# Two intermediate tensors re-laid by six-channel groups across all images, and the last pass issued in halves instead of thirds

## The chip, the cores and the metric

The kernel runs on one core of one Trainium2 chip. Its metric is the device time of one execution in microseconds (us); the kernel before took a median of 6009.42 us in three runs (6007.35 to 6020.1).

## The reference

Two residual layers over an image batch `x` of shape (8, 96, 96, 192), all in float32. `_gn` is a group norm with 32 groups of six channels.

```python
# layer 0
proj  = x_gn @ W_in + b_in                      # 192 -> 384
local = conv3x3_depthwise(proj)
mixed = 0.25 * (lr + rl + tb + bt) + local      # four running means (s = 0.6 s + 0.4 x) over rows and columns
x     = x + layernorm(mixed) @ W_out + b_out    # 384 -> 192
# layer 1
y = conv7x7_depthwise(_gn(x)) + dw_bias
y = layernorm(y)
y = gelu(y @ w0 + b0) @ w1 + b1                 # 192 -> 768 -> 192
x = x + y * gamma
```

The output has the shape of `x`.

## The kernel before

The work runs in five stages, one after the other, with intermediate tensors in DRAM between them. The order of instructions on every engine is the order in which the code issues them; each stage is written out inside a manual schedule.

- **A, projection** (to line 528): group norm of `x` and the 192 to 384 projection; the result goes to `P_d`. On the side it prepares shifted copies of the convolution kernels (`Z1_d`, `Z2_d`) and writes one row of zeros (`pad`, line 298) behind the end of `X1_d`.
- **B, 3x3 convolution and running means** (lines 540 to 683); result in `M_d`.
- **C, layer norm and output projection** (lines 765 to 982): 192 steps `u`. `load_c` (line 807) loads `mt` and `xr` on SP's queue; `block_c` runs TensorE; `finish_c` (line 851) forms the new `x` (called x1), stores it in token order to `X2_d` on POOL's queue and copies it into `x1c`, in channel-major order. When sixteen steps are done, `x1c` holds, for two images and one of three column phases, 96 rows of all 192 channels; sixteen calls of `store_c` (line 926) write it to `X1_d` on SP's queue, twelve channels each, one call per following step. At the end one store is made, then `load_d(0)` is issued, and then the other fifteen stores.
- **D, 7x7 convolution** (lines 991 to 1083): sixteen groups `i` of twelve channels. A tile `m` holds six channels of all images for three pairs of row blocks: `load_d` (line 738) loads `xin`, its lower 64 partitions on SP's queue and its upper 64 on POOL's, and `band`, the shifted kernel, in the same way. Five tiles `xin` exist in turn. `scale_d` (line 1004) applies the second group norm on VectorE, eight instructions a tile. `conv_d` (line 1011) does the convolution as banded matmuls of 63 rows and 64 columns, four of them side by side in TensorE's array, and ScalarE adds the bias into `yo`. `store_d` (line 1043) writes `yo` to `Y_d` in sixteen transfers on POOL's queue (in the last group, the first image pair's part goes to SP's queue).
- **E, layer norm and the two-layer network** (lines 1093 to 1270): 96 units `u` of four columns of two images, 96 rows each. `load_y` (line 1113) loads `Y_d` on SP's queue once in four units; `load_r` (line 1118) loads the residual from `X2_d`; `stats_e` and `norm_e` are the layer norm on VectorE; `turn_in(u, k)` (line 1163) transposes on TensorE into `pt` and copies to `yT` on VectorE; `first_layer(u, mb)` (line 1177) multiplies with `w0w`; `second_layer(u, k)` (line 1209) multiplies with `w1g`, adds the residual on VectorE and stores to the output on POOL's queue.

The contraction over 192 channels in `first_layer` is done as one matmul over 128 rows (line 1186) and one over 64 rows (line 1196); the two halves of a unit's tokens use the upper and the lower 64 rows at the same time. ScalarE then applies GELU (line 1205). Each call of `first_layer` does two of six output blocks, `ms = (2 * mb, 2 * mb + 1)`, and so four PSUM tiles `hp`. PSUM is shared out as two `pt`, four `hp` and two `po`.

The order of E around the change, for each unit `u`:

```python
for k in range(3):
    first_layer(u, k)
    turn_in(u + 1, k)
    ...                      # loads, statistics and norm of u + 2 on VectorE
    second_layer(u - 1, k)
```

The layouts that the change touches: `X1_d` is (image pair, row and column phase; channel; column; image of the pair), so that one partition of `xin` reads four runs of 1536 bytes, one per image pair. `Y_d` is (row and phase; image pair, half; channel; column and image), so that one partition of `yo` writes eight runs of 768 bytes, and one partition of `y` reads one run of 24,576 bytes.

Of the kernel before, what the change touches and what calls it, by code (L numbers as in the profile page):

```python
# [8 lines left out]
F32 = mybir.dt.float32  # L9
# [75 lines left out]
def conv_blocks_kernel(  # L85
# [31 lines left out]
    nc = tc.nc  # L117
# [24 lines left out]

    X1_d = dram.tile([BP * S * PH + 1, D, WV, 2], F32, name="X1_d")
    X2_d = dram.tile([BP, PH, S, WV, 2, D], F32, name="X2_d")
    NV = 2
    WQ = WV // NV

    Y_d = dram.tile([S * PH, BP, NV, D, 2 * WQ], F32, name="Y_d")

# [71 lines left out]
    with ExitStack() as ph:  # L221
# [30 lines left out]
        k1t = zp.tile([S, 2, 7, 7], F32, name="k1t")  # L252
        pad = zp.tile([S, D * WV * 2 // S], F32, name="pad")

# [35 lines left out]
        def store_kernels():  # L290
            nc.sync.dma_start(
                Z0_d.rearrange("(m p) t l -> p m (t l)", p=128),
                z0.rearrange("p m t l -> p m (t l)"),
            )

            nc.sync.dma_start(Z1_d.rearrange("(i c) p l -> c i p l", c=S), z1)
            nc.sync.dma_start(
                X1_d[BP * S * PH].rearrange("(i c) v b -> i (c v b)", i=S), pad
            )
# [430 lines left out]
    HG = HB - 6  # L730
    HC = GS
    CD = 2 * HC
# [5 lines left out]
    def load_d(m):  # L738
        c = m * HC
        row = D * WV * 2  # L740
        pool = d_pools[m % ND > 0]
        xin = pool.tile([128, NT, BP, HC, 2 * WV], F32, tag="xin", name="xin")

        for t in range(NT):
            for g, eng in enumerate((nc.sync, nc.gpsimd)):
                src = bass.AP(
                    tensor=X1_d.tensor,
                    offset=X1_d.offset + (2 * t + g) * HG * PH * row + c * WV * 2,
                    ap=[[row, 64], [S * PH * row, BP], [1, HC * WV * 2]],
                )  # L750
                eng.dma_start(
                    xin[g * 64 : (g + 1) * 64, t].rearrange("q a c n -> q a (c n)"), src
                )
        band = pool.tile([128, HC, ZW], F32, tag="band", name="band1")
        for g, eng in enumerate((nc.sync, nc.gpsimd)):
            eng.dma_start(
                band[g * 64 : (g + 1) * 64].rearrange("q c l -> q (c l)"),
                Z2_d[:, c : c + HC].rearrange("r c l -> r (c l)"),
            )
        return band, xin  # L760
# [4 lines left out]
    with ExitStack() as ph:  # L765
# [160 lines left out]
        def store_c(x1c, k, q):  # L926
            c = slice(q * D // NX, (q + 1) * D // NX)
            bp, p = divmod(k, NH)
            r = bp * S * PH
            nc.sync.dma_start(X1_d[r + p : r + S * PH : PH, c], x1c[:, c])  # L930

# [59 lines left out]
    with ExitStack() as ph:  # L991
# [51 lines left out]
        def store_d(yo, i):  # L1043
            for bl in range(NB):
# [6 lines left out]
                for k in range(2):  # L1051
                    c = i * CD + k * HC
                    for lo, hi in pieces:
                        r = (S - HB - bl * HG) * PH
                        src = yo[k * 64 + lo * PH : k * 64 + hi * PH, bl]
                        dst = Y_d[r + lo * PH : r + hi * PH, :, :, c : c + HC].rearrange(
                            "r b a c n -> r (b a) (c n)"
                        )
                        src = src.rearrange("r a c n -> r a (c n)")

                        n = NV if i == D // CD - 1 else 0
                        if n:
# [28 lines left out]


    WH = 4
    WE = 2 * WH
    HE = 128 // WH
    with ExitStack() as ph:
        ip = ph.enter_context(tc.tile_pool(name="e_in", bufs=2))
        sp = ph.enter_context(tc.tile_pool(name="e_small", bufs=3))
        tp = ph.enter_context(tc.tile_pool(name="e_t", bufs=2))
        ps_t = ph.enter_context(tc.tile_pool(name="e_ps_t", bufs=2, space=PSUM))  # L1100
        ps_h = ph.enter_context(tc.tile_pool(name="e_ps_h", bufs=4, space=PSUM))
        ps_o = ph.enter_context(tc.tile_pool(name="e_ps_o", bufs=2, space=PSUM))

# [9 lines left out]
        def load_y(n):  # L1113
            bp, p, a = place(n)
            ys[n] = ip.tile([S, D, 2 * WQ], F32, tag="y", name=f"y_{n}")
            nc.sync.dma_start(ys[n], Y_d[PH - 1 - p :: PH, bp, a])

# [59 lines left out]
        def first_layer(u, mb):  # L1177
            if mb == 0:
                gs[u] = tp.tile([128, NE, 2, WH * S], F32, tag="g", name="g")
            yT, g = yTs[u].rearrange("p k h j -> p k (h j)"), gs[u]  # L1180
            ms = (2 * mb, 2 * mb + 1)
            hps = {}
# [26 lines left out]
        def second_layer(u, k):  # L1209
            if k == 0:  # L1210
                xos[u] = tp.tile([128, S // HE, 2, D], F32, tag="xo", name="xo")
            g, xo = gs[u], xos[u]
            po = ps_o.tile([128, 2, D], F32, tag="po", name="po")
            for q in range(2):
# [24 lines left out]
        with tc.manual_schedule():  # L1239
# [10 lines left out]
            for u in range(n_u + 1):  # L1250
                for k in range(3):
                    if u < n_u:
                        first_layer(u, k)
                    if u + 1 < n_u:
                        turn_in(u + 1, k)
                    if k == 0:
                        if u + 1 < n_u:
                            load_r(u + 1)
                        if u < n_u:
                            bias_r(u)  # L1260
                    if u + 2 < n_u:
                        if k < 2:
                            for j in range(4 * k, 4 * k + 4):
                                stats_e(u + 2, j)
                        else:
                            for j in range(WE):
                                norm_e(u + 2, j)
                    if u >= 1:
                        second_layer(u - 1, k)

# [46 lines left out]
```

## Time and profile before

The profiled execution took 6011.68 us, its span (first to last instruction) 6009.9 us. The three runs have a median of 6009.42 us.

| engine | busy us | share of the span |
|---|---|---|
| TensorE matmul (PE) | 5680.5 | 95% |
| TensorE weight load (PEld, beside PE) | 3943.4 | 66% |
| VectorE (DVE) | 3454.0 | 57% |
| POOL | 2634.7 | 44% |
| ScalarE (ACT) | 2440.3 | 41% |

| stage | us from the span's start | us |
|---|---|---|
| A | 0 to 782 | 782 |
| B | 782 to 1835 | 1053 |
| C | 1835 to 2924 | 1089 |
| change-over from C to D | 2924 to 3014 | 90 |
| D | 3014 to 3501 | 487 |
| from D to E | 3501 to 3546 | 45 |
| E and its tail | 3546 to 6010 | 2464 |

The stages' bounds are read off TensorE's timeline, so they are good to a few us. How to read the views that follow: a *group* line gives source line, engine, operation, output<-input and how often; a *wait* line says who waited for whom, total us, times, longest; a *timeline* line gives the start, the time and a run of like instructions, and in brackets how long the engine was idle before it and what ended that. TensorE is pipelined, so the distance between starts says more than the busy time. `X_d` in the profile stands for both `X1_d` and `X2_d`. DMA transfers go through queues: q0 is POOL's, q1 is SP's; all queues share sixteen DMA engines.

### The profile page before, as it was taken

To read this page: it belongs to the slowest core of one execution; us is meant where nothing else is said; L and a number is where in the kernel's file an instruction comes from. 1 tells how busy PE (TensorE), PEld (TensorE's weight loads), DVE (VectorE), ACT (ScalarE), POOL (GpSimd) and SP (SyncE) were. 2 spreads that over 40 slices of the span, in tenths; PEclk is the share of its full clock that TensorE was granted. 3 is DMA by queue.
4 is the path that set the end of the run, shared out by engine and by line. 5 is a ranking of instruction groups with operands and counts; after the bars stand their busy time and mean duration, and the time that the engine had idled before them with its cause. 6 is when DMAs were issued, how large, how long until landed. Compare 5 with 4: busy or idle time off the path is not lost.

```text
span 6009.9 us, 122810 instructions
## 1 busy us (share of the span) xinstructions
PE 5680.5 (95%) x48550; PEld 3943.4 (66%) x48550; DVE 3454.0 (57%) x8023; ACT 2440.3 (41%) x6146; POOL 2634.7 (44%) x2835
## 2 busy tenths in 40 slices
PE   6999989999998999999677769999999999999999
PEld 3655633333336989898666657777777777777777
DVE  5555469999995667777532334444444444444442
ACT  2444457777774555555333322222222222222221
POOL 1111148888886666666444422322332233233222
PEclk9999989999999999999888889999999999999999
DMA  7999779999987888888899952222222222222221
GB/s 206 282 285 258 219 213 243 244 242 244 244 231 210 266 261 268 262 267 261 232 286 290 284 141 69 66 72 63 79 64 78 64 79 64 78 64 77 61 64 37
DMA packets 570206, 1054.36 MB, mean 175 GB/s; under 512 B 109575, under 2 KB 426260, under 8 KB 567328
## 3 DMA queue, kind: packets, MB, share of 16 engines
q1 hardware_dynamic: 439344, 593.23, 37.8%
q0 software_dynamic: 124160, 450.67, 24.1%
q8 instruction: 384, 6.29, 0.5%
q10 hardware_dynamic: 6128, 2.61, 0.2%
q14 instruction: 190, 1.56, 0.1%
HBM read 585.19 MB, written 476.57 MB: 177 GB/s over the span
## 4 chain that ended last, share of the span: by engine, by line
PE 77%; DMA 6%; DVE 1%; issue 1%; SPq 1%; POOL 1%; ACT 0%; DVEq 0%; POOLq 0%; ACTq 0%
PE po L1216 19%; PE po L833 13%; PE hp L1186 12%; PE pl L579 10%; PE hp L1196 7%; PE pa L600 5%; PE pt L831 4%; DMA xin<-X_d 4%; PE py L1024 2%; PE pt L1169 2%; PE pa L603 2%; DMA Y_d<-yo 1%; DVE xin L1009 1%; DMA band<-Z_d 0%; SPq L1063 0%
## 5 line engine op out<-in xcount | busy, mean ns | idle before, releaser
L1205 ACT ACTIVATE g<-hp,b0g 128x384 f32<-128x384 f32 x1152 | 573.9, 580 | 1856.4 <-PE hp L1196 1856.4
L1216 PE MATMUL po<-w1g,g 128*128 128x192 f32 x6912 | 1178.3, 327 | 0.0
L1216 PEld LDWEIGHTS po<-w1g,g 128*128 128x128 f32 x6912 | 1116.6, 190 | 1.6 <-issue 1.1
L833 PE MATMUL po<-wc,mt 128*96 128x193 f32 x4608 | 912.8, 333 | 0.0
L1173 DVE COPY yT<-pt 128x384 f32<-128x384 f32 x288 | 251.4, 873 | 1126.7 <-PE pt L1169 1126.4
L1234 POOL DMA_DIRECT2D out_dram<-xo x576 | 321.3, 560 | 1147.9 <-DVE xo L1223 1119.4
L1186 PE MATMUL hp<-yT,w0w 128*128 128x384 f32 x2304 | 794.4, 488 | 0.4 <-ACT g L1205 0.4
L833 PEld LDWEIGHTS po<-wc,mt 128*96 128x96 f32 x4608 | 701.8, 163 | 68.6 <-ACT mean L837 65.0
L579 PE MATMUL pl<-pin,band 34*32 34x380 f32 (+1 forms) x13824 | 629.9, 489 | 19.3 <-DMA pin<-P_d 18.5
L1186 PEld LDWEIGHTS hp<-yT,w0w 128*128 128x128 f32 x2304 | 431.4, 191 | 231.6 <-issue 2.6
L609 DVE TENSOR_TENSOR_SCAN z<-decay,loc 128x768 f32<-128x768 f32 x288 | 505.9, 1756 | 61.2 <-ACT loc L588 31.7
L1024 PE MATMUL py<-xin,band 63*64 63x248 f32 (+1 forms) x6912 | 405.5, 394 | 138.3 <-DVE xin L1009 136.2
L649 POOL TENSOR_TENSOR mo<-mo,z 128x768 f32<-128x768 f32 x288 | 529.6, 1839 | 3.3 <-ACT mo L604 0.4
L618 DVE TENSOR_TENSOR_SCAN z<-decay,z 128x768 f32<-128x768 f32 x288 | 498.2, 1730 | 0.0
L579 PEld LDWEIGHTS pl<-pin,band 34*32 34x32 f32 x13824 | 232.8, 107 | 398.7 <-issue 397.1
L1024 PEld LDWEIGHTS py<-xin,band 63*64 63x64 f32 x6912 | 345.0, 142 | 198.5 <-DVE xin L1009 123.5
L840 ACT ACTIVATE sq<-pt,mean 96x384 f32<-96x384 f32 x768 | 443.0, 577 | 25.7 <-ACT mean L837 0.8
L1196 PE MATMUL hp<-yT,w0w 64*128 64x384 f32 x2304 | 449.4, 508 | 0.0
L600 PE MATMUL pa<-loc,mix 128*32 128x384 f32 x3456 | 431.9, 493 | 0.0
L603 PE MATMUL pa<-last,down 96*32 96x384 f32 x1152 | 426.9, 493 | 0.9 <-ACT mo L604 0.9
L29 POOL TENSOR_TENSOR rs<-rs_ve,neg_half 96x8 f32<-96x8 f32 x96 | 158.6, 1652 | 606.3 <-DVE rs_ve L28 606.3
L362 PE MATMUL pm<-xT,win 128*128 128x384 f32 x1152 | 395.9, 494 | 3.3 <-DVE po L386 3.3
(116 smaller groups left out, 7707.4 us busy)
## 6 DMA issues: line engine op xcount, KB each, us to landing
P_d<-po POOLq DMA_DIRECT2D x96, 1152.0 KB, 9.9
pin<-P_d SPq DMA_DIRECT2D x192, 576.0 KB
mt<-M_d SPq DMA_DIRECT2D x576, 192.0 KB
xq<-in_x_dram SPq DMA_DIRECT2D x96, 576.0 KB
xr<-in_x_dram SPq DMA_DIRECT2D x384, 144.0 KB
X_d<-x1u POOLq DMA_DIRECT2D x192, 288.0 KB, 4.2
X_d<-x1c SPq DMA_DIRECT2D x192, 288.0 KB
y<-Y_d SPq DMA_DIRECT2D x24, 2304.0 KB
```

The lines of the kernel that those rows point to most:

```text
L579: nc.tensor.matmul(pls[g][at * RB : (at + 1) * RB, :, lo:hi], band[rows, c, kh, :], pin[rows, c, :, NJ - 1 - j, lo + kh - 1 : hi + kh - 1] ...
L600: nc.tensor.matmul(pa[at], mix[:, i, at], loc[:, q], start=True, stop=True)
L603: nc.tensor.matmul(pa[at], down[:, to], last[:, q], start=True, stop=True)
L609: nc.vector.tensor_tensor_scan(zf, decay_f, loc.rearrange("p q n -> p (q n)"), 0.0, ALU.mult, ALU.add)
L618: nc.vector.tensor_tensor_scan(zr, decay_f, zr, 0.0, ALU.mult, ALU.add)
L649: nc.gpsimd.tensor_tensor(m, m, z, ALU.add)
L833: nc.tensor.matmul(po[:S, b], lhs[m], wc[:, m], start=(m == 0), stop=(m == NC - 1))
L1024: nc.tensor.matmul(pys[t // 2][g][k * 64 : (k + 1) * 64, t % 2, :, lo:hi], pair[k][0][rows, c, d * ZS : d * ZS + 64], pair[k][1][rows, t, ...
L1186: nc.tensor.matmul(hps[m, q], w0w[:, 2 * q, m * 128 : (m + 1) * 128], yT[:, 2 * q], start=True, stop=False,)
L1196: nc.tensor.matmul(hps[m, q], w0w[p, 1, m * 128 : (m + 1) * 128], yT[p, 1], start=False, stop=True,)
L1205: nc.scalar.activation(g[:, m, q], hps[m, q], AF.Gelu, bias=b0g[:, m : m + 1], scale=1.0)
L1216: nc.tensor.matmul(po[:, q], g[:, m, q, k * 128 : (k + 1) * 128], w1g[:, m], start=(m == 0), stop=(m == NE - 1),)
```

## The change

Both intermediate tensors get the layout (row and phase; group of six channels; image pair; ...), so that for one row and one group of six channels the values of all images lie together in DRAM, 6144 bytes. A tile `xin` then reads one run of 6144 bytes per partition, and `yo` writes one. `store_c` writes two runs of 1536 bytes per row where it wrote one of 3072, and `load_y` reads 32 runs of 768 bytes per partition. The numbers of transfers and the bytes stay as they were, except for the row of zeros, which is four times as long.

In the last pass `first_layer` does three of the six output blocks in a call and is called twice a unit, not three times. PSUM is shared out anew: one `pt`, and seven buffers in turn for both `hp` and `po`. The order per unit is written out by hand: first half, transposes 0, second layer 0, transposes 1, second half, transposes 2, second layer 1, second layer 2.

```diff
-    X1_d = dram.tile([BP * S * PH + 1, D, WV, 2], F32, name="X1_d")
+    HC = GS
+    X1_d = dram.tile([S * PH + 1, D // HC, BP, HC, WV, 2], F32, name="X1_d")
...
-    Y_d = dram.tile([S * PH, BP, NV, D, 2 * WQ], F32, name="Y_d")
+    Y_d = dram.tile([S * PH, D // HC, BP, NV, HC, 2 * WQ], F32, name="Y_d")
...
-        pad = zp.tile([S, D * WV * 2 // S], F32, name="pad")
+        pad = zp.tile([S, D * WV * B // S], F32, name="pad")
...
-        row = D * WV * 2
+        row = D * WV * B
...
-                    offset=X1_d.offset + (2 * t + g) * HG * PH * row + c * WV * 2,
-                    ap=[[row, 64], [S * PH * row, BP], [1, HC * WV * 2]],
+                    offset=X1_d.offset + (2 * t + g) * HG * PH * row + c * WV * B,
+                    ap=[[row, 64], [1, HC * WV * B]],
...
-            r = bp * S * PH
-            nc.sync.dma_start(X1_d[r + p : r + S * PH : PH, c], x1c[:, c])
+            nc.sync.dma_start(
+                X1_d[p : S * PH : PH, c.start // HC : c.stop // HC, bp].rearrange(
+                    "h g c v b -> h g (c v b)"
+                ),
+                x1c[:, c].rearrange("h (g c) v b -> h g (c v b)", c=HC),
+            )
...
-                        dst = Y_d[r + lo * PH : r + hi * PH, :, :, c : c + HC].rearrange(
-                            "r b a c n -> r (b a) (c n)"
+                        dst = Y_d[r + lo * PH : r + hi * PH, c // HC].rearrange(
+                            "r b a c n -> r (b a c n)"
                         )
-                        src = src.rearrange("r a c n -> r a (c n)")
-
-                        n = NV if i == D // CD - 1 else 0
+                        src = src.rearrange("r a c n -> r (a c n)")
+
+                        n = NV * HC * 2 * WQ if i == D // CD - 1 else 0
...
-        ps_t = ph.enter_context(tc.tile_pool(name="e_ps_t", bufs=2, space=PSUM))
-        ps_h = ph.enter_context(tc.tile_pool(name="e_ps_h", bufs=4, space=PSUM))
-        ps_o = ph.enter_context(tc.tile_pool(name="e_ps_o", bufs=2, space=PSUM))
+        ps_t = ph.enter_context(tc.tile_pool(name="e_ps_t", bufs=1, space=PSUM))
+        ps_h = ph.enter_context(tc.tile_pool(name="e_ps_h", bufs=7, space=PSUM))
...
-            nc.sync.dma_start(ys[n], Y_d[PH - 1 - p :: PH, bp, a])
+            nc.sync.dma_start(
+                ys[n].rearrange("h (g c) n -> h g (c n)", c=HC),
+                Y_d[PH - 1 - p :: PH, :, bp, a].rearrange("h g c n -> h g (c n)"),
+            )
...
-            ms = (2 * mb, 2 * mb + 1)
+            ms = range(mb * NE // 2, (mb + 1) * NE // 2)
...
-            po = ps_o.tile([128, 2, D], F32, tag="po", name="po")
+            po = ps_h.tile([128, 2, D], F32, tag="hp", name="po")
...
-                for k in range(3):
-                    if u < n_u:
-                        first_layer(u, k)
-                    if u + 1 < n_u:
-                        turn_in(u + 1, k)
...
-                    if u >= 1:
-                        second_layer(u - 1, k)
+                if u < n_u:
+                    first_layer(u, 0)
+                if u + 1 < n_u:
+                    turn_in(u + 1, 0)
+                    load_r(u + 1)
+                if u < n_u:
+                    bias_r(u)
+                if u + 2 < n_u:
+                    for j in range(4):
+                        stats_e(u + 2, j)
+                if u >= 1:
+                    second_layer(u - 1, 0)
+                if u + 1 < n_u:
+                    turn_in(u + 1, 1)
+                if u < n_u:
+                    first_layer(u, 1)
+                if u + 1 < n_u:
+                    turn_in(u + 1, 2)
+                if u + 2 < n_u:
+                    for j in range(4, WE):
+                        stats_e(u + 2, j)
+                if u >= 1:
+                    second_layer(u - 1, 1)
+                if u + 2 < n_u:
+                    for j in range(WE):
+                        norm_e(u + 2, j)
+                if u >= 1:
+                    second_layer(u - 1, 2)
```

## The prediction

> **What bounds the kernel now.** I first read the profiled execution by stage, as a table of engine busy time in stretches: projection, 3x3 convolutions, output projection with the norm (C), then the change-over into the 7x7 convolution, that convolution (D), its end, and the last pass (E) with its tail.
>
> ```profile
> 1835.00:2924.00 1089.00, 1074.75 (x6931) 972.98 (x6932) 752.94 (x2657) 630.95 (x2300) 720.94 (x577) 0.99 0.87 259
> 2924.00:3014.00 90.00, 35.34 (x474) 31.68 (x474) 41.38 (x123) 13.86 (x29) 19.80 (x32) 0.66 0.89 225
> 3014.00:3501.00 487.00, 379.58 (x6476) 321.65 (x6476) 134.37 (x225) 188.23 (x359) 218.57 (x342) 0.87 1.01 278
> 3501.00:3546.00 45.00, 3.29 (x13) 2.09 (x14) 9.26 (x28) 0.68 (x2) 11.16 (x17) 0.52 0.86 202
> 3546.00:5978.00 2432.00, 2426.43 (x12548) 1808.30 (x12549) 1112.38 (x2944) 573.23 (x1149) 722.13 (x757) 1.00 0.24 68
> ```
>
> Columns: stretch and its us, busy time of PE, PEld, DVE, ACT and POOL, TensorE clock, DMA share, GB/s. C and E are TensorE's (1075 of 1089 us, 2426 of 2432). D is not: TensorE is busy 380 of 487 us, at a clock of 0.87, and the DMA engines are full at 278 GB/s.
>
> For D I read the waits and then one period in the timelines of POOL, DVE and PE.
>
> ```profile
> DVE xin L1009 <- DMA xin<-X_d: 329.3, 28, 23.4
> PE py L1024 <- DVE xin L1009: 109.5, 15, 10.7
> POOL Y_d L1064 <- DMA xin<-X_d: 75.1, 56, 2.5
> ```
> ```profile
> 3206.60 0.70 POOL L1064 DMA_DIRECT2D Y_d<-yo  x1 [2.83 <-ACT yo L1035]
> ...
> 3230.46 1.31 POOL L751 DMA_DIRECT2D xin<-X_d  x2 [0.76 <-PE py L1024]
> ```
> ```profile
> 3244.91 4.74 DVE L1009 TENSOR_SCALAR xin<-xin,s 128x576 f32<-128x576 f32 x8 [20.75 <-DMA xin<-X_d]
> ```
> ```profile
> 3216.65 24.78 PE L1024 MATMUL py<-xin,band 63*64 63x256 f32 x432 [9.74 <-DVE xin L1009]
> 3249.71 25.23 PE L1024 MATMUL py<-xin,band 63*64 63x256 f32 x432 [8.28 <-DVE xin L1009]
> ```
>
> TensorE loses 8 to 10 us before each group of twelve channels, because a group's second tile arrives late. The convolution before last ended at 3206.9. Its 16 stores are first in POOL's queue and take until 3230.5, since each POOL transfer waits for the eighth before it (the built program shows eight semaphores used in turn); only then does POOL ask for its half of the next tile, which is there at 3244.9; DVE normalizes for 4.8; TensorE starts at 3249.7. So 23.6 + 14.4 + 4.8 = 42.8 us from one end to the start after next, with a convolution of 25 inside: (42.8 + 25)/2 = 33.9 us per group, against 33.1 measured.
>
> For E I read TensorE's timeline in the steady state.
>
> ```profile
> 4011.38 2.74 PE L1186 MATMUL hp<-yT,w0w 128*128 128x384 f32 x8
> 4014.06 1.56 PE L1196 MATMUL hp<-yT,w0w 64*128 64x384 f32 x8
> 4015.55 0.55 PE L1169 MATMUL pt<-ident,yn 96*128 96x96 f32 x4
> 4015.93 4.09 PE L1216 MATMUL po<-w1g,g 128*128 128x192 f32 x24
> 4019.86 0.49 PE L1186 MATMUL hp<-yT,w0w 128*128 128x384 f32 x1
> ```
>
> A third of a unit takes 8.48 us, a unit 25.44, 96 units 2442. Single starts in the same trace: full-height matmuls follow each other by 0.322, the 64-row pairs by 0.316, transposes by 0.082; but from the last full one to the first pair it is 0.416, from the first pair to the second 0.420, from the last pair to the first transpose 0.413, and from that to the second 0.139. Each visit to the 64-row matmuls thus costs 0.094 + 0.104 + 0.097 + 0.057 = 0.35 us.
>
> **The Trainium skill.** "TensorEngine Tiling (Array Packing)", Key Properties, says that changing the tiling mode drains TensorE: the 0.09 to 0.10 us steps agree. "SBUF — State Buffer", Door 1, says that partitions 0 to 63 reach only eight of sixteen ports and 64 to 127 the other eight: the trace agrees, since POOL's half of a tile, alone in the stretch 3235 to 3241, moves at 208 GB/s, and stores together with SP's loads reach 404 at 3227 to 3230. "DMA: Bandwidth & Descriptors", Why small descriptors are slow, speaks of a fixed cost per packet: packets of 1536 B take 68 ns undisturbed and of 4992 B 198, so about 10 ns each beyond the bytes. Its Latency section says that HBM rows spaced by large powers of two slow DMA; no run here shows that yet (it returns as a rival).
>
> **The change part by part.**
>
> *Last pass in halves (L1181, L1250).* The same matmuls, in two groups of three output blocks instead of three of two: two visits to the 64-row mode per unit instead of three. One transpose group now stands between a second-layer group and the first layer, both full-height, where I see no drain: a transposes-to-full step costs 0.03 today and is kept. Gain 0.33 us x 96 = 32 us, all on the path. New waits: 7 buffers serve 6 `hp` and 3 `po` in turn, and `pt` has one. A buffer comes back seven tiles later: for the first half these are GELUs of the half before, done 4 us earlier (6 x 0.50 us on ACT after the block, against 7.9 us of second layer); for the second half, GELUs 4.7 us of other matmuls away. The single `pt` waits for a DVE copy of 0.87 us with 3.9 us of second layer between. DVE has about 13 us of work per 25. So these cost nothing; if the cover fails, one stall of about 1 us per unit would cost 96 and I bound it there; below, the gain can't exceed the 0.35 x 96 = 34.
>
> *D's loads (L748) in 6 KB runs instead of four of 1.5 KB.* Same bytes, a quarter of the descriptors, still on the same 64 partitions. From the trace's packet records, 6 KB takes 4 x 68 = 272 ns on SP's queue, and 4608 + 1536 B = 376 + 140 = 516 ns for POOL's half alone (port bound). With 4992 B at 198 and 386 ns as the nearest rows, 6144 B should take 245 and 475: 10% and 8% less.
>
> *D's stores (L1056) in 6 KB runs instead of eight of 768 B.* POOL's queue packs those already into packets of 4608 + 1536 B: 188 + 67 = 255 ns, against 247: 3%.
>
> Together: the store stretch of 23.6 us carries stores and SP's loads in about equal parts, so 6.5% or 1.5 us; POOL's load of 14.4 us gives 1.1. The latency loop shortens by 2.6, the group by 1.3, over 14 groups 18 us. If instead the full DMA engines are what counts, the packet times of the whole stage fall by 6%, 29 us. I take 24. The number of transfers and their eight-deep turn are unchanged, so POOL's issue of about 0.65 us each stays hidden behind landing. What is late next is still POOL's half tile.
>
> *Change-over 2924 to 3014.* Loads from both halves together run there at 281 GB/s, 1536 B in 101 ns and 4992 B in 272; a tenth less of some 57 us of loading is -5.5. The 15 last stores of x1 (13 us) now write 1536 B instead of 3072 (2 x 68 against 121 ns, +12%): +1.5. Together -4.
>
> *C's other x1 stores on SP.* 192 of 288 KB: 18,432 packets more at some 7 ns, spread over sixteen engines, about 15 us of DMA time against a stage with 13% of DMA time free and TensorE 99% busy: nothing. Were `mt` to come late for it, at most +13.
>
> *E's y loads (L1116)*, 24 on SP, ahead of `r` loads in its queue: 3072 runs of 768 B instead of 96 of 24 KB. Packets of 768 B take 36 to 42 ns in C, so 192 per engine are 7 to 8 us, against 13 for the first load now (2304 KB at about 230 GB/s). If descriptors came no faster than C's 205 per us, 15. In steady state a load has four units, 100 us. At E's start it is on the path: -5 to +3; I take 0. The pad (48 to 192 KB, in the first stage, behind TensorE) is nothing.
>
> Sum: -32 - 24 - 4 = -60. The profiled execution took 6011.7 us (span 6009.9), 2.3 above the median of the runs shown, so 5951.7 there and 5949 by the median.
>
> **The rivals.** (a) *D doesn't move*: its pace is set by ports and by the eight-deep turn. For it: 208 GB/s is a port figure, and the stores were packed already. Against: the 8 and 10% per packet are measured. 6009 - 32 = 5977. (b) *D falls to TensorE's pace*: fewer descriptors let SP's loads start earlier (now they move almost nothing for six us after issue), gaps shrink below those at which the clock sags, and a group takes 27 us: 14 x 6 = 84; 6009 - 32 - 84 - 5 = 5888. Against: bytes per group (9.5 MB) at 27 us need 353 GB/s on average, where the best stretches make 404. (c) *E gains nothing* (a hidden turn of buffers stalls as much as is saved): 6009 - 28 = 5981. (d) *Slower: HBM rows.* Neighbouring partitions of a tile were 48 KB apart in x1 and are now 192 KB apart, and engines 768 KB. If that lowers the loads' rate, the 14.4 and the 23.6 us grow. It decides once a group costs 60/14 = 4.3 us more than I forecast, that is loads slower by about a fifth; at half rate, POOL's load alone adds 14 us to the loop, 7 per group, and with SP's about 10: 14 x 10 - 32 = +108, 6117. Against: Y is stored today with a row pitch of 192 KB at full rate, and y's loads at 576 KB do 14 B/ns per engine, like the first stage's x loads at 72 KB pitch (15.5).
>
> **How the numbers follow.** Forecast 0.50 (own range 5930 to 5968), (a) 0.17, (b) 0.15, (c) 0.08, (d) 0.07, and 0.03 for a small loss in D that cancels E. Faster by over 0.2% (12 us, about what measurement can tell from no change): 0.90; same 0.03; slower 0.07. The range goes down to (b) and up past (c): 5886 to 5990, with (d) and part of (b) outside.
>
> **What would show it.** E's unit 25.1 us instead of 25.44, with two 0.416 steps per unit; no PE waits on ACT or DVE there. POOL's packets of 6144 B at 475 ns alone; groups in D 31 to 32 us apart; TensorE's wait before each group still 6 to 8 us and still ended by DVE behind `xin`. I am wrong if groups come faster than 29 us (b), not faster than 33 (a), or slower (d), and if TensorE waits in E (c).

## The result

| | median of its runs, us | ratio to before, 95% interval |
|---|---|---|
| before, in the same comparison | 6012.9 | 1 |
| after | 5966.4 (5962.9 to 5971.1) | 0.9923 [0.9905, 0.994] |

The kernel is 46 us faster, where I forecast 60 and 5949. The profiled execution took 5971.1 us with a span of 5969.3, so the two traces differ by 40.6 us of span. Read off TensorE's timeline, that is

| part of the span | before | after | difference |
|---|---|---|---|
| A, B, C, up to D's first matmul | 2963.6 | 2965.5 | +2.0 |
| D, first matmul to last | 537.3 | 533.5 | -3.8 |
| from there to E's first transpose | 40.6 | 38.1 | -2.5 |
| E and the end | 2468.4 | 2432.2 | -36.2 |

So the last pass paid, and the re-laid tensors hardly did: the time went down as forecast, but not where it was forecast. The table by stage, to be held against the one of before (stretch and its us; busy time of PE, PEld, DVE, ACT, POOL; TensorE clock, DMA share, GB/s):

```profile
1835.00:2924.00 1089.00, 1073.29 (x6918) 971.74 (x6919) 750.90 (x2652) 629.78 (x2295) 719.03 (x576) 0.99 0.87 259
2924.00:3014.00 90.00, 45.13 (x612) 39.17 (x614) 48.24 (x137) 17.19 (x37) 20.21 (x35) 0.70 0.85 243
3014.00:3499.00 485.00, 372.47 (x6356) 308.72 (x6348) 129.31 (x216) 185.93 (x354) 180.15 (x340) 0.86 0.95 275
3499.00:3537.00 38.00, 0.01 (x1) 0.00 (x0) 5.15 (x19) 0.84 (x3) 9.41 (x17) 0.54 0.90 210
```

C is as it was: the stores of x1 in shorter runs cost TensorE nothing. D is as it was too: 275 GB/s where it was 278, TensorE busy 372 us where it was 380, at nearly the same granted clock (0.86 for 0.87). Only the DMA engines' share fell, from 1.01 to 0.95: the packets got cheaper, and TensorE was not served sooner. The waits inside D, in the same stretch:

```profile
DVE xin L1015 <- DMA xin<-X_d: 331.1, 27, 29.3
...
PE py L1030 <- DVE xin L1015: 112.5, 14, 16.7
POOL Y_d L1070 <- DMA xin<-X_d: 104.0, 62, 2.8
```

VectorE still waits 330 us for loads, and TensorE 110 us for VectorE. One period, first in POOL's timeline, then in DVE's and PE's:

```profile
3269.94 0.53 POOL L1070 DMA_DIRECT2D Y_d<-yo  x1 [1.82 <-ACT yo L1041]
...
3294.89 0.50 POOL L1070 DMA_DIRECT2D Y_d<-yo  x1 [0.73 <-DMA Y_d<-yo]
3296.06 1.03 POOL L753 DMA_DIRECT2D xin<-X_d  x2 [0.67 <-DMA Y_d<-yo]
```
```profile
3305.96 4.74 DVE L1015 TENSOR_SCALAR xin<-xin,s 128x576 f32<-128x576 f32 x8 [19.77 <-DMA xin<-X_d]
```
```profile
3277.80 26.07 PE L1030 MATMUL py<-xin,band 63*64 63x256 f32 x432 [7.55 <-DVE xin L1015]
3310.75 24.97 PE L1030 MATMUL py<-xin,band 63*64 63x256 f32 x432 [6.88 <-DVE xin L1015]
```

The chain has the same links as before. Its sizes moved: the stores now take until 3296.06 (26 us instead of 23.6), POOL's half tile is then there after 10 us (instead of 14.4). What one link gained the other lost.

The change-over ahead of D's steady state did come out shorter. The third group's line, of before and of after:

```profile
3047.55 25.60 PE L1024 MATMUL py<-xin,band 63*64 63x256 f32 x431 [8.04 <-DVE xin L1009]
```
```profile
3047.21 25.32 PE L1030 MATMUL py<-xin,band 63*64 63x256 f32 x432 [16.73 <-DVE xin L1015]
```

TensorE was through with the second group 9 us earlier (3030.5 for 3039.5), and then waited 9 us longer: the third starts at 3047 in both.

E's steady state, TensorE's timeline over one unit and the first line of the next:

```profile
4006.84 4.06 PE L1195 MATMUL hp<-yT,w0w 128*128 128x384 f32 x12
4010.83 2.21 PE L1205 MATMUL hp<-yT,w0w 64*128 64x384 f32 x12
4012.97 0.55 PE L1178 MATMUL pt<-ident,yn 96*128 96x96 f32 x4
4013.36 7.99 PE L1225 MATMUL po<-w1g,g 128*128 128x192 f32 x48
4021.19 4.03 PE L1195 MATMUL hp<-yT,w0w 128*128 128x384 f32 x12
4025.15 2.21 PE L1205 MATMUL hp<-yT,w0w 64*128 64x384 f32 x12
4027.29 0.55 PE L1178 MATMUL pt<-ident,yn 96*128 96x96 f32 x4
4027.67 4.09 PE L1225 MATMUL po<-w1g,g 128*128 128x192 f32 x24
4031.60 0.50 PE L1178 MATMUL pt<-ident,yn 96*128 96x96 f32 x4
4031.93 4.06 PE L1195 MATMUL hp<-yT,w0w 128*128 128x384 f32 x12
```

A unit takes 4031.93 - 4006.84 = 25.09 us, where it took 25.44, with two lines of 64-row matmuls and no bracket: TensorE waits for nobody here. The single starts at a visit are still 0.416, 0.420, 0.413 and 0.139 us apart; there are two visits instead of three.

### The profile page after: what moved, and what is told of

Read it like the earlier page. It is cut to its first block, busy times and chain, and to the rows that moved or that the text cites. A ratio compares the mean times of both kernels' runs of the same rounds, so it can differ in the third digit from the quotient of the medians.

```text
span 5969.3 us, 122712 instructions
## 1 busy us (share of the span) xinstructions
PE 5648.3 (95%) x48550; PEld 3955.4 (66%) x48550; DVE 3451.9 (58%) x8023; ACT 2429.6 (41%) x6146; POOL 2612.4 (44%) x2835
## 4 chain that ended last, share of the span: by engine, by line
PE 78%; DMA 5%; DVE 1%; issue 1%; POOL 1%; SPq 0%; ACT 0%; POOLq 0%; DVEq 0%; ACTq 0%
PE po L1225 19%; PE po L835 14%; PE hp L1195 12%; PE pl L582 10%; PE hp L1205 7%; PE pa L603 5%; PE pt L833 4%; PE py L1030 4%; PE pa L606 2%; DMA xin<-X_d 2%; PE pt L1178 2%; DMA Y_d<-yo 2%; DVE xin L1015 1%; DMA X_d<-x1c 0%; SPq L1069 0%
## 5 line engine op out<-in xcount | busy, mean ns | idle before, releaser
L1225 PE MATMUL po<-w1g,g 128*128 128x192 f32 x6912 | 1160.0, 327 | 0.0
L1195 PE MATMUL hp<-yT,w0w 128*128 128x384 f32 x2304 | 780.5, 489 | 0.4 <-DVE yT L1182 0.4
L1243 POOL DMA_DIRECT2D out_dram<-xo x576 | 341.7, 595 | 876.4 <-DVE xo L1232 842.9
L1205 PE MATMUL hp<-yT,w0w 64*128 64x384 f32 x2304 | 423.5, 500 | 0.0
```

The costliest lines, as they stand in the source:

```text
L1195: nc.tensor.matmul(hps[m, q], w0w[:, 2 * q, m * 128 : (m + 1) * 128], yT[:, 2 * q], start=True, stop=False,)
L1205: nc.tensor.matmul(hps[m, q], w0w[p, 1, m * 128 : (m + 1) * 128], yT[p, 1], start=False, stop=True,)
L1225: nc.tensor.matmul(po[:, q], g[:, m, q, k * 128 : (k + 1) * 128], w1g[:, m], start=(m == 0), stop=(m == NE - 1),)
```

## The experiments

All ratios are to the kernel before, in the same comparison. "D" is D's first matmul to its last, "E" E's first transpose to the end, both from the one profiled execution of each kernel. Runs of one kernel spread over 8 us and more (e3: 5944 to 5962), so a few us between two D or E are within what a single profile can tell.

| kernel | median us | ratio [95%] | D us | E us |
|---|---|---|---|---|
| after | 5966.4 | 0.9923 [0.9905, 0.9940] | 533.5 | 2432.2 |
| e1, layouts only | 5994.0 | 0.9963 [0.9951, 0.9976] | 525.8 | 2461.8 |
| e2, halves only | 5988.0 | 0.9957 [0.9944, 0.9971] | 540.2 | 2442.0 |
| e13, halves and Y only | 5975.7 | 0.9936 [0.9922, 0.9949] | 543.9 | 2431.9 |
| e3, queues alternate halves | 5950.7 | 0.9895 [0.9882, 0.9909] | 523.8 | 2434.9 |
| e4, D's loads on SP | 5898.3 | 0.9809 [0.9796, 0.9822] | 467.7 | 2432.1 |
| e5, e4 with the old layouts | 5997.7 | 0.9971 [0.9960, 0.9983] | 565.2 | 2431.8 |
| e12, e4 with x1 new, Y old | 5890.3 | 0.9793 [0.9778, 0.9808] | 449.3 | 2432.0 |
| e6, e4 with band on POOL | 5918.1 | 0.9835 [0.9820, 0.9849] | 479.0 | 2435.0 |
| e11, e4 with band on ScalarE's queue | 5901.1 | 0.9809 [0.9793, 0.9825] | 466.5 | 2435.4 |
| e9, e4 in transfers of 32 rows | 5935.2 | 0.9872 [0.9857, 0.9887] | 495.2 | 2434.6 |
| e7, 128 partitions a transfer, SP | 7143.1 | 1.1872 [1.1854, 1.1889] | | |
| e8, 128 partitions, tiles by queue | 6577.0 | 1.0931 [1.0914, 1.0947] | | |

### The two parts apart

e1 has both new layouts and the last pass of before: the pools and the loop of before are put back. e2 has the new last pass and both old layouts.

```diff
# e1, against after; e2, against before, the other way round
-        ps_t = ph.enter_context(tc.tile_pool(name="e_ps_t", bufs=1, space=PSUM))
-        ps_h = ph.enter_context(tc.tile_pool(name="e_ps_h", bufs=7, space=PSUM))
+        ps_t = ph.enter_context(tc.tile_pool(name="e_ps_t", bufs=2, space=PSUM))
+        ps_h = ph.enter_context(tc.tile_pool(name="e_ps_h", bufs=4, space=PSUM))
+        ps_o = ph.enter_context(tc.tile_pool(name="e_ps_o", bufs=2, space=PSUM))
...
-            ms = range(mb * NE // 2, (mb + 1) * NE // 2)
+            ms = (2 * mb, 2 * mb + 1)
```

> The changed kernel with the last pass of the kernel before (thirds, two pt, four hp, two po). If the two parts add and the last pass brought 33 to 36 us of the 46, this one is 10 to 13 us faster than before (ratio about 0.998). If the re-laid tensors brought the 28 us that I forecast for the 7x7 stage and its change-over, and the last pass less than it seems, it is 25 to 30 us faster. If the parts help each other (y loads of 768-byte runs disturb the old order of the last pass), it is as slow as before or slower.

> The kernel before with the last pass of the changed one and the old layouts. If the gain is one visit less to the 64-row matmuls per unit, 0.34 us in each of 96 units, it is 33 us faster (ratio 0.9945), and a unit takes 25.10 us. If part of the 36 us seen in that stage came from the new y loads, it is less, down to 30.

e1 is 22 us faster than before, e2 26 to 28; together about the 46 of the whole, so the two parts add up. E's unit stays at 25.44 us in e1 and is 25.09 in e2: it belongs to the halves alone. In e1's trace the layouts gave 11.5 us in D, 2.4 between D and E, and 6.7 at the kernel's end. That last piece is hardly the layouts'. It lies in a closing instruction of POOL, a drain that starts when the last outputs are issued: it takes 9.65 us in before and e2, 2.5 to 3.0 in ten of the others, 5.9 in e6 and 7.5 in e8. e5, further down, has e2's layouts and 2.5. Why is open. The trace records instruction fetches of 8 KB near the end (q14 in the profile), but the one in before has landed 6 us before the drain ends, and the last one starts after the last instruction, so no trace shows that the drain waits for them. So e1's 22 us hold 7 that the layouts were not shown to bring. e2's E is 26.4 us shorter than before: 33.3 for the units, less 6.9 that the pass's start and its last units take longer in the new order (3.8 in after).

### Why D doesn't follow its packets

To see what each queue moves, I cut D's middle (3090 to 3400 us) into half microseconds and sorted them by which queues had packets. GB/s:

| kernel | both queues: share of time, POOL + SP = sum | POOL alone | SP alone |
|---|---|---|---|
| before | 70%, 200 + 125 = 325 | 30%, 204 | 1% |
| e2 | 67%, 198 + 129 = 327 | 32%, 207 | 1% |
| e13 | 67%, 202 + 124 = 326 | 30%, 206 | 3%, 222 |
| after | 53%, 161 + 170 = 331 | 47%, 245 | 0% |
| e1 | 50%, 160 + 173 = 332 | 50%, 242 | 0% |
| e3 | 52%, 165 + 175 = 340 | 47%, 256 | 0% |
| e5 | 61%, 157 + 142 = 299 | 0% | 39%, 217 |
| e4 | 78%, 159 + 202 = 362 | 0% | 22%, 245 |
| e12 | 91%, 137 + 216 = 353 | 5%, 210 | 4%, 253 |

From how many GB/s on a queue counts as having packets is a choice, and with others the sum of before comes out at 314 to 341. The totals in the DMA lines further down are free of it.

With 6 KB runs SP's queue moves 170 GB/s beside POOL's instead of 125, and POOL's 161 instead of 200; the sum hardly changes. SP has 3.0 MB to bring in a group (half of two tiles), POOL 6.5 (the other half and 3.5 MB of stores). Before: SP is done after 3.0/0.125 = 24 us, POOL has then moved 4.8 MB and needs 1.75/0.204 = 8.6 more: 32.6. After: 3.0/0.170 = 17.6 us, POOL has moved 2.8 and needs 3.7/0.245 = 15.1 more: 32.7. The traces have 33.1 and 32.8 from group to group. The gain went to the queue that nobody waits for. The DMA part of the profile over the same stretch (packets, MB, share of sixteen engines) says so in three lines, of before and of after:

```profile
DMA packets 35444, 90.12 MB, mean 291 GB/s; under 512 B 5810, under 2 KB 21360, under 8 KB 35406
...
q0 software_dynamic: 18684, 61.55, 73.3%
q1 hardware_dynamic: 16722, 28.00, 30.4%
```
```profile
DMA packets 20592, 90.58 MB, mean 292 GB/s; under 512 B 5466, under 2 KB 5466, under 8 KB 20553
...
q0 software_dynamic: 14564, 61.99, 72.1%
q1 hardware_dynamic: 5989, 28.00, 26.7%
```

41% fewer packets, 292 GB/s for 291. SP's packets (q1) need a smaller share of the engines, POOL's (q0) almost the same. And once SP is done, POOL's half tile comes at the rate it always had; after, 3234 to 3242 us:

```profile
DMA packets 360, 1.67 MB, mean 209 GB/s; under 512 B 76, under 2 KB 76, under 8 KB 360
...
q0 software_dynamic: 360, 1.67, 102.1%
```

209 GB/s with runs of 6144 bytes, where the same phase of before showed 208 with 1536. A packet of 6144 bytes takes 476 ns there, as forecast (475). But the forecast set it against one packet of 4608 bytes and one of 1536, 516 ns. POOL's queue joins three runs where it can, and of sixteen it makes five packets of 4608 and one of 1536 (e13's records from 3090 to 3400 us, with the same loads: 4320 and 864), which at 374 and 140 ns are 502 ns for 6144 bytes. So these packets got 5% cheaper, not 8, and those of `band` not at all: with all that POOL loads, 80 ns per KB for 81 to 83.

The two terms of the loop, as means over all groups in D's middle: from the end of a convolution to POOL's first load it takes 22.1 us in before and in e2, 25.9 in after and e1; from there to the next convolution's start 19.3 and 19.2, and 14.8 and 14.9. So stores got 3.8 us longer, as SP moved more beside them, and the load 4.5 shorter, as SP was through by then. The loop lost 0.7 us of 41.

e13 asks which tensor does it, with the queues of after: only Y is re-laid.

```diff
# against after
-    X1_d = dram.tile([S * PH + 1, D // HC, BP, HC, WV, 2], F32, name="X1_d")
+    X1_d = dram.tile([BP * S * PH + 1, D, WV, 2], F32, name="X1_d")
...
-                    ap=[[row, 64], [1, HC * WV * B]],
+                    ap=[[row, 64], [S * PH * row, BP], [1, HC * WV * 2]],
...
```

> After, with x1 and its loads in the layout of before: only Y has the new one (the queues are those of after). Theory 'shares': a queue's share beside the other goes with the length of its packets; in D of before POOL moved 199 GB/s and SP 125 side by side, of after 161 and 170, with nearly the same sum, and a group ends when POOL has moved its stores and its half tiles. With stores of 6144 bytes against loads of 1536, SP gets 100 to 115 and POOL 210 to 225: SP's 3 MB take 27 to 29 us, in which POOL has done about 6 of its 6.5 MB, so a group takes 30 to 31.5 us instead of 32.7, and the time is 15 to 35 us below after: 5931 to 5951. Rival 'ports alone' (the sum is set by ports, the order by the queues, the shares don't count): a group of 32.7 and 5960 to 5975, as after. Rival 'SP becomes the late one': SP's share falls so far that its half tile comes last, a group of 33 us or more, 5970 to 5990.

5976, D at 543.9 and shares as in before: this half of my theory of shares fell. Longer store packets didn't give POOL more. A part of the reason may be that POOL's queue had joined its 768-byte runs to packets of 4608 and 1536 bytes already; but the same step goes with more for POOL between e12 and e4 below (137 and 159), so it stays open. D with the old x1 (before, e2, e13) is 540 us on the mean, with the new one (after, e1) 530. Kernels of these with the same x1 lie up to 8 us apart, and the medians of e13 and after have intervals that overlap. So whatever D gained, some 4 to 11 us, is little more than these runs can tell; it came with x1, whose loads on SP got faster.

### Who waits behind whom

e3 and e4 change only which queue carries the loads. In e3 POOL's half is the lower and the upper in turn; in e4 POOL has the stores alone.

```diff
# e3, against after
-            for g, eng in enumerate((nc.sync, nc.gpsimd)):
+            for g in range(2):
+                eng = (nc.sync, nc.gpsimd)[(g + t) % 2]
...
-        for g, eng in enumerate((nc.sync, nc.gpsimd)):
+        for g, eng in enumerate((nc.gpsimd, nc.sync)):
```
```diff
# e4, against after (for xin and for band)
-            for g, eng in enumerate((nc.sync, nc.gpsimd)):
+            for g, eng in enumerate((nc.sync, nc.sync)):
```

> The changed kernel, where SP's and POOL's queue take the lower and the upper 64 partitions of a tile in turn, from one block pair to the next; transfers, bytes and packets as they were. If POOL's half tile, which runs alone at 203 to 205 GB/s for some 14 of 33 us, is held by the ports of its 64 partitions, mixing the halves in one queue lets it run faster, as the stores do that alternate halves (366 GB/s alone): up to 5 us per group of twelve channels, 30 to 70 us in all. If all DMA engines step through the halves together, or if the eight-deep turn and the landing set the pace, nothing changes (within 5 us of the changed kernel).

> The changed kernel with all loads of the 7x7 stage on SP's queue, the stores alone on POOL's. If the pace is the loop (stores ahead of the loads in POOL's queue, then the load, then the normalization), the loop falls to about 25 us and the stage to TensorE's pace: 7 us per group, about 100 us in all. If ports are the bound, 6.0 MB of loads per group through one queue, one half at a time at about 195 GB/s, take 31 us beside the stores: a group takes 30 to 31 us, 25 to 40 us in all. If the bound is the number of transfers in flight per queue (eight), SP now has sixteen loads per group instead of eight and a group takes as long as now or longer.

e3 gives 16 us, between its two forecasts, of which D 10: POOL's lone load, now of both halves in turn, runs at 220 to 260 GB/s instead of 209. That one half is slow by itself is so part of the matter, and the smaller part. e4 gives 68 us over after and 118 over before, again between its forecasts (100, and 25 to 40). A group takes 28.6 us instead of 32.8. Its waits between 3065 and 3434 us:

```profile
DVE xin L1015 <- DMA xin<-X_d: 202.2, 21, 11.7
...
PE py L1030 <- DVE xin L1015: 49.4, 13, 5.9
```

In the same stretch after has 84.1 us in 11 waits of TensorE, so it is 3.8 us a group instead of 7.6. The loads no longer stand behind the stores in POOL's queue, so both queues are at work for 78% of the time instead of 53. What is late now is SP's queue: its loads wait 215 us of the stretch for earlier ones of their own to land, and 0.2 us for TensorE to free a tile.

### What the long runs are worth there

e5 is e4 with both layouts of before. e12 is e4 with only x1 re-laid.

```diff
# e12, against e4
-    Y_d = dram.tile([S * PH, D // HC, BP, NV, HC, 2 * WQ], F32, name="Y_d")
+    Y_d = dram.tile([S * PH, BP, NV, D, 2 * WQ], F32, name="Y_d")
...
-                        dst = Y_d[r + lo * PH : r + hi * PH, c // HC].rearrange(
-                            "r b a c n -> r (b a c n)"
+                        dst = Y_d[r + lo * PH : r + hi * PH, :, :, c : c + HC].rearrange(
+                            "r b a c n -> r (b a) (c n)"
...
```

> The layouts of before, the last pass in halves, and all loads of D on SP's queue. It asks what the 6 KB runs are worth once D's loads no longer queue behind its stores. Theory 'ports and order' (D is set by half tiles that are port bound and by what queues behind what; the length of the runs hardly counts): a group takes 28.5 to 29.5 us as with the new layouts, and the time is within 15 us of e4_loads_on_sp, so 5900 to 5920. Theory 'packets' (descriptors of 1536 B cost about 10 ns more each, and SP's queue, unlike POOL's, doesn't pack them): SP's loads then run 10% slower, a group takes 31 us, and the time is 5930 to 5945.

> As e4_loads_on_sp, but only x1 has the new layout; Y is stored and read as before (runs of 768 bytes, which POOL's queue packs). With both old layouts and the loads on SP it was 5998, with both new ones 5898. Theory 'the loads': SP's packets of 6144 bytes hold their own beside POOL's, those of 1536 don't, so x1 alone gives nearly all of the 100: 5895 to 5915, and 5 to 7 us of it is the end of the kernel, where the new layouts finish sooner. Rival 'the stores': the packing of POOL's short runs costs on the way, and x1 alone gives half: 5940 to 5960.

e5 went past both theories: 5998. e2, which has the same layouts and loads on two queues, is at 5988 (the two intervals overlap), with 540 us in D. e5's D takes 565 us where e4's takes 468. So the 6 KB runs that were worth 4 to 11 us in the change itself are worth 97 us of D when the queue that carries them is the one TensorE waits for. The DMA part of both, 3090 to 3400 us, first e5, then e4:

```profile
DMA packets 41503, 83.39 MB, mean 269 GB/s; under 512 B 5344, under 2 KB 32846, under 8 KB 41467
...
q1 hardware_dynamic: 31635, 52.75, 64.5%
q0 software_dynamic: 9832, 30.10, 33.2%
```
```profile
DMA packets 23793, 104.75 MB, mean 338 GB/s; under 512 B 6288, under 2 KB 6288, under 8 KB 23749
...
q1 hardware_dynamic: 13932, 65.24, 64.8%
q0 software_dynamic: 9817, 38.84, 34.5%
```

With the same share of the engines, 64.5 and 64.8%, SP's queue brought 52.8 MB in the one and 65.2 in the other.

e12 gave 5890, below its own range of 5895 to 5915: the loads' layout carries all of it, none of it at the kernel's end, which is as in e5, and the new Y rather costs D something (449 us against 468; in the two medians 8 us, whose intervals just overlap). It is the fastest version that I ran, 2.1% below before. Its D in TensorE's timeline:

```profile
3224.01 24.60 PE L1030 MATMUL py<-xin,band 63*64 63x256 f32 x432 [3.49 <-DVE xin L1015]
3251.11 24.70 PE L1030 MATMUL py<-xin,band 63*64 63x256 f32 x432 [2.51 <-DVE xin L1015]
3279.81 25.70 PE L1030 MATMUL py<-xin,band 63*64 63x256 f32 x432 [4.00 <-DVE xin L1015]
```

The brackets, 8 to 10 us in before, are 2.5 to 4. Beside POOL's packets of 4608 and 1536 bytes SP's get 216 GB/s, beside those of 6144 in e4 202. "DMA: Bandwidth & Descriptors" of the Trainium skill, Queues, rings and completion order, says that each DMA engine serves the queues in turn, a packet at a time. What SP's queue moves agrees in direction (125 to 170, and 142 to 202, as its packets grew, and 202 to 216 as POOL's shrank), not in size: in e5 POOL's packets are 1.8 times as long as SP's on the mean (30.10 MB in 9832 and 52.75 in 31635), and POOL moves 1.1 times as much beside it. e13 against e2, 124 and 129, is too small a step to count for or against it.

### What limits D then

e6 moves only the loads of `band` to POOL, e11 to ScalarE's queue; e9 cuts SP's transfers of xin.

```diff
# e6, against e4
-        for g, eng in enumerate((nc.sync, nc.sync)):
+        for g, eng in enumerate((nc.gpsimd, nc.gpsimd)):
```
```diff
# e11, against e4
-        for g, eng in enumerate((nc.sync, nc.sync)):
+        for g, eng in enumerate((nc.scalar, nc.scalar)):
```
```diff
# e9, against e4
-            for g, eng in enumerate((nc.sync, nc.sync)):
+            for h, g in ((0, 0), (0, 1), (1, 0), (1, 1)):
...
-                    ap=[[row, 64], [1, HC * WV * B]],
+                    ap=[[row, 32], [1, HC * WV * B]],
```

> After, with all of xin on SP's queue and all of band (1.28 of 6 MB a group) on POOL's, where it stands behind the stores of the group before. Theory 'SP's queue of loads sets the pace of D': a group's loads on SP shrink by a fifth, from 28.6 to about 23 us, TensorE's 25 us becomes the bound, a group takes 25.5 to 26.5, and the time is 30 to 40 us below e4_loads_on_sp: 5860 to 5870. Rival 'the sixteen DMA engines or the ports are full': the bytes are the same, so 28.6 stays: 5890 to 5905. Rival 'order': band arrives last, behind the stores, as POOL's half tile did: a group of 30 to 33 us, 5920 to 5966.

> As e4_loads_on_sp, with band on ScalarE's queue, a third one that waits behind no store. If D is paced by how much SP's queue carries, and shares with the stores are by queue, the loads gain a share: a group 26 to 27.5 us, 5870 to 5890. If the sixteen engines are the limit at about 360 GB/s with two queues or three, nothing moves: 5893 to 5903. If ScalarE's activations wait behind the issue of the loads, TensorE waits for PSUM: 5905 to 5930.

> As e4_loads_on_sp (all loads on SP), with each xin transfer cut into two of 32 rows, the four of a step alternating between the halves of the partitions. The bytes, the run length and the queues stay. In e4_loads_on_sp SP's queue alone moves 245 GB/s for 22% of the time, and both queues together 362. Theory 'ports': two halves that alternate more finely keep both sets of ports in use, SP's queue alone rises to 300 or more, and the time falls by 5 to 20 us from e4_loads_on_sp: 5880 to 5893. Rival 'one queue alone is limited otherwise' or 'issue': SP issues 28 transfers a group instead of 16 and is the later for it: 5898 to 5930.

e6 came out between its two rivals, at 5918. TensorE starts a group, does two matmuls and waits again, now for `band`:

```profile
3219.85 0.61 PE L1030 MATMUL py<-xin,band 63*64 63x256 f32 x2 [1.94 <-issue]
3222.57 24.64 PE L1030 MATMUL py<-xin,band 63*64 63x256 f32 x430 [2.11 <-DMA band<-Z_d]
```

It is the wait of before in small: the 1.28 MB of `band` stand behind the stores. e11 takes them out of both queues and is 5901, D 466.5, as e4; over D's middle three queues move 345 GB/s, two 338. That is as forecast if the sixteen engines together, not the length of one queue, set D; what else could hold it at that level was not tried. e9 fell on the rival's side and came out slower still than its range: cut finer, SP's queue alone is hardly faster (254 GB/s for 245), and it is alone 38% of the time instead of 22. That the 28 issues a group make SP late is likely, but not shown by itself; between 3065 and 3434 us its loads have 103 us of waits before they are issued, in e4 215.

### An experiment that measured something else

e7 and e8 were to load all 128 partitions of a step in one transfer, on SP alone or a tile per queue.

```diff
# e7, against e4 (e8: eng = (nc.gpsimd, nc.sync)[m % 2])
-                    ap=[[row, 64], [1, HC * WV * B]],
+                    ap=[[HG * PH * row, 2], [row, 64], [1, HC * WV * B]],
...
```

> As e4_loads_on_sp (all loads on SP), but each of the three transfers of an xin tile covers all 128 partitions, not 64 (band stays in two). Theory 'ports': a transfer to 64 partitions alone is port bound at 200 to 240 GB/s; over 128 it runs at 300 or more while no store is under way, a group takes 25.5 to 27 us, and the time is 20 to 40 us below e4_loads_on_sp: 5860 to 5880. Rival 'one queue has its own limit near 230 GB/s' or 'HBM side': 28.6 us and 5890 to 5905 as in e4_loads_on_sp.

> As after, with the same bytes on each queue in the same order, but the queues take whole tiles in turn (even tiles POOL, odd ones SP), each xin transfer over all 128 partitions. So POOL still loads behind its stores and is alone then, but reaches both halves of the ports. Theory 'POOL's load is port bound': its 14 us at 203 GB/s become 8 to 10 us at 300 or more, the loop over two groups loses 4 to 6 us, a group 2 to 3, and the time is 28 to 42 us below after: 5925 to 5938. Rival 'order and the eight-deep turn alone count, or POOL's descriptors are slow whatever the partitions': within 8 us of after, 5958 to 5974.

Neither theory saw this: 7143 and 6577 us. The DMA part of e7, 3215 to 3240 us (the first line is the engines' busy share in 40 slices, in tenths):

```profile
DMA  1111111111111111111111111111111111111988
GB/s 49 49 59 49 49 59 49 49 49 59 49 49 59 49 49 59 49 49 49 59 49 49 59 49 49 59 49 49 59 49 49 59 49 49 59 49 57 195 303 140
DMA packets 289, 1.61 MB, mean 64 GB/s; under 512 B 15, under 2 KB 15, under 8 KB 289
```

A share of 0.13 of sixteen engines is the time of two engines (3100 to 3110 us: 53 GB/s at 0.13), with 234 ns for 6144 bytes, as where nothing else is under way. "DMA: Bandwidth & Descriptors" of the Trainium skill, Rules for kernel authors, says that an outermost dimension smaller than sixteen confines a transfer to at most that many engines; the source's outermost dimension here is 2, and the trace agrees. So e7 and e8 say nothing on ports.

## Why the prediction was right, and where it was wrong

*The last pass.* Right, in mechanism and size: (25.440 - 25.093) x 96 = 33.3 us for a forecast of 32, and no wait of TensorE in the steady state. Between two full-height groups the transposes cost what I had kept: behind them the second full matmul starts 0.35 us after the first, where the others follow by 0.32. Not in my sum were E's start and last units in the new order (+4) and the 7 us at the kernel's end, which no part of the change was shown to bring. These 7 are luck: without them the time would be some 5973, outside the 5930 to 5968 that I gave the forecast itself, and near rival (a).

*D.* The step that failed is "Together: the store stretch of 23.6 us carries stores and SP's loads in about equal parts, so 6.5% or 1.5 us; POOL's load of 14.4 us gives 1.1". The packets did get cheaper (SP's 6 KB in 234 ns undisturbed, against 4 x 68; POOL's alone in 476, against 502 and not the 516 of my sum), but I took each queue's part of the stretch to shrink by its own percentage. The stretch got 3.8 us longer, the load 4.5 us shorter, and the loop lost 0.7 instead of 2.6. With the change-over my -24 - 4 became -4 in this pair of traces and -11 on the mean of all kernels with those queues. Rival (a) described D best, 5977 in all, though for a reason that it had only in part: the port-like 208 GB/s stayed, but what held D was that the time saved fell to the other queue.

*The bounds.* The rows 192 KB apart (rival d) did no harm: 26.3 B/ns per engine undisturbed. E's first y load, taken at nothing between -5 and +3, takes 14.0 us from its issue to the first statistics where it took 13.2, so it gained nothing. The gap before E is shorter all the same, 38.1 to 38.3 us in every kernel with the new Y and 40.0 to 40.7 with the old, since the last stores, ahead of that load in SP's queue, are through sooner: it is issued 16.7 us behind D's last matmul instead of 20.1. C's stores and the pad cost nothing, as taken; the 15 us of DMA time in that sum should have been 8 (18,432 packets at 7 ns on sixteen engines), and C's DMA share is 0.87 in both. Rival (b), D near TensorE's pace, is nearly reached with other queues, and the change alone doesn't reach it: it needs the loads out of POOL's queue as well (28.6 us a group in e4, for some 25 of matmuls). As the waits shrank, the granted clock between 3065 and 3400 us rose, from 0.86 in after to 0.92 in e4 and 0.94 in e12.

*Open.* Why a queue that only loads stops at 204 to 254 GB/s, while POOL's stores alone reach 350 to 381 at 3295 to 3297 us in after. The ports of half the partitions fit POOL's 209 and the 220 to 260 with both halves in e3, but a finer alternation added nothing in e9, and the full-width transfer ran on two engines. How many transfers a queue has in flight (eight, by the eight semaphores that POOL's and SP's transfers take in turn) was not varied by itself. Open too is why Y's new layout costs D rather than helps it; that was seen in two pairs (e13 against e2, +4 us; e4 against e12, +18), each profiled once. For the second the shares above fit, SP's 202 for 216.

## What to carry to other kernels

In these runs cheaper packets helped the queue that sent them. Ask first which queue's last byte the kernel waits for, and work out both queues' finishing times, because what one gains beside the other can be the other's loss. When a stage's loads stand behind its stores in one queue, take them out of it before making them cheaper: the same 6 KB runs were worth some 10 us of D at most with the old queues and 97 with the loads by themselves. And look at the outermost dimension of a transfer: with one of 2, e7 took 7143 us where e4 took 5898.

## What the runs showed of the hardware that I had not expected

- Two queues side by side moved 325 to 332 GB/s in all five kernels with stores and one half of the loads on POOL and the other half on SP, whatever the packets; with loads and stores on queues of their own 299 with packets of 1536 bytes and 362 with 6144.
- One half of the partitions loaded by POOL's queue alone: 204 to 209 GB/s, with 1536 as with 6144 bytes a run.
- A transfer whose source begins with a dimension of 2: 49 to 59 GB/s, at the busy time of two engines.
- POOL's queue joins short runs (768 and 1536 bytes) to packets of 4608 and 1536; SP's sends those of 1536 as they are.
- POOL's closing drain takes 2.5 to 9.65 us behind the last outputs, with no change to those outputs.
